# Gram chains of images 1 to 5: which engine runs the small operations (four convolution layers on one Trainium2 core)

## The chip, the cores and the metric

The kernel runs on one core of a Trainium2 chip. Its engines each have their own queue of instructions: TensorE (PE in the profile) multiplies matrices, VectorE (DVE) and ScalarE (ACT) work element by element, GpSimd (POOL) does so too and starts DMAs, SyncE (SP) starts most DMAs. The metric is the device time of one execution in microseconds (us); the smaller the better. Times are medians of several runs.

## The reference

The input `x` is 16 images of 64 channels of 128 x 128 pixels, in float32. Four layers follow each other, each with a group normalization `_gn` (32 groups of two channels) and an addition to its own input:

```python
def _L0_conv_ref(x, conv_w):
    xf = x.reshape(B, C, N)
    gram = jnp.einsum('bcn,bdn->bcd', xf, xf) / N
    y = jnp.einsum('bcd,bdn->bcn', gram, xf)
    out = jnp.einsum('oc,bchw->bohw', conv_w, y)
...
x = x + _L0_conv_ref(_gn(x), L0_conv_conv_w)            # a 64 x 64 Gram matrix of each image
x = x + _L1_conv_ref(_gn(x))                            # |Sobel x| + |Sobel y| of each channel
x = x + _L2_conv_ref(_gn(x), L2_conv_W, L2_conv_b)      # 3x3 convolution after a shift by a column
x = x + _L3_conv_ref(_gn(x), w_bin, w1x1, ...)          # 3x3 and 1x1, batch norm, leaky ReLU, clip
```

The batch norm of the last layer takes its mean over all 16 images, so its end can only be computed when all images are through.

## The kernel before, in words

One partition of the chip's memory stands for a channel of one half of an image (64 channels x upper and lower half = 128 partitions). Layer 0 is linear in `x`: once the Gram matrix of an image is known, normalization, Gram product, 1x1 weights and the residual become one 64 x 64 matrix `abd` and a few columns `co`. So an image passes through these stages:

- `Gram` (L407): loads the whole image (`xr`), rearranges it on ACT (`xw`), and sums 128 small products on PE into `pg`, a 64 x 65 Gram matrix with the channel sums.
- `gram_chain` (L301): about forty small operations on 128x1 to 128x128 tiles that turn `pg` into `abd` and `co`. It alternates between DVE, which computes, and PE, which sums over partitions by small products into one PSUM tile, `bank`.
- `Front`: applies `abd` (`po`), normalizes on ACT (`xh`), and does layer 1's Sobel filters on DVE: eight operations of about 1000 elements a step, with two absolute values (`Abs`, in place on `u` and `e`) on ACT between them.
- `Layer2` and `Layer3`: the convolutions on PE (`one`, `two`), differences `d` of rows and the final additions on DVE (`two`, `x`, `y`), twins `qd` of the differences. In layer 2, POOL starts the DMAs that make `qd`, scales the edge columns (`edges`, four operations) and zeroes columns of `v` (two operations); DVE's next `d` needs that `v`.
- at the end, 16 images are read again, normalized by the batch norm, added and written. This end is bound by DMA.

The stages run at the same time on different images. The program writes out the order by hand: a loop over steps, each in four quarters `q`, and in each quarter it calls the stages in turn (Layer3, Layer2, Front, Gram). At the end of the quarter `tick()` advances the chains: a chain is a generator, and each `yield` ends a link, so that a link's products on PE wait for operations that were queued one quarter earlier. Image 1's chain has fewer breaks (`if b > 1: yield`), so that some of its products stand right behind the operations that they need.

Every instruction goes into its engine's queue in the order in which the program names it, and the wrapper `InOrder` forbids the scheduler to move it:

```python
def __getattr__(self, name):
    call = getattr(self.engine, name)
    def ordered(*args, **kwargs):
        return self.tc.keep_in_program_order(call(*args, **kwargs))
    return ordered
```

Because of this wrapper nearly all instructions carry line L73, and the profile is read by tile names.

The Gram stages of images 1 to 6 run at double pace (`half`, L874), while the pipeline still fills: image 0's chain falls at 38 us, that of image b at step 12 + 4b, and layer 2 joins at step 23, layer 3 at step 34. `EARLY` is 3. The links that matter, with the queue that they stand in:

- `gs`: copy of `pg`, in the quarter in which ACT copies the first two `xw` pieces of the next image.
- `vv`: five columns made of the mean `mu` of a channel and the group's `mean` (the latter in `me`); PE's next product `bank<-kc,vv` reads them.
- `rw`: copy of a 2 x 256 product out of PSUM.
- `rc`: the 1x1 weights times `r`; `cs`: sums of PSUM and `g`; PE multiplies `rc` by `cs`.
- `r2`, `wbd` (in two 64 x 64 halves), `ad`, `abd`: they make the matrix; in the profile `r2` appears as `r<-r`.
- `co`: five small operations that make the columns for `Front`.

Of the kernel before, what the change touches and what calls it, by code (L numbers as in the profile page):

```python
# [12 lines left out]
ALU = mybir.AluOpType  # L13
# [9 lines left out]
EARLY = 3  # L23
# [85 lines left out]
def tile_kernel(ctx: ExitStack, tc: tile.TileContext, x, cw_h, w2_t, b2, wbin_t, w1_t, b1, gamma, beta, consts, out):  # L109
    nc = tc.nc  # L110
    pe, dve, act, sp, pool = (InOrder(tc, e) for e in (nc.tensor, nc.vector, nc.scalar, nc.sync, nc.gpsimd))
# [9 lines left out]
    def k(name):  # L121
        return kc[:, AT[name][0]:AT[name][1]]

    def load_const(src, shape, name):
        t = cpool.tile(shape, F32, name=name)
        nc.sync.dma_start(t, src)
        return t

    cwh = load_const(cw_h, [P, C], "cwh")
# [39 lines left out]
    def sv(name, n=1):  # L169
        return small.tile([P, n], F32, tag=name, name=name)  # L170
# [6 lines left out]
    def small_product(dst, wt, src):  # L177

        for o in (1 - last[0], last[0]):
            pe.matmul(dst[cols(o)], wt[:, cols(o)], src, start=True, stop=True)  # L180
        last[0] = o
# [5 lines left out]
    def sm(n, rows=P):  # L187
        if n > 8:
            return bank[0:rows, P:P + n]
        turn[0] = (turn[0] + 1) % 16  # L190
        return bank[0:rows, 8 * turn[0]:8 * turn[0] + n]
# [9 lines left out]
    wbd = wpool.tile([P, P], F32, name="wbd")  # L201
# [55 lines left out]
    def rstd(mE, eps):  # L257

        me = sv("me", 2)
        dve.tensor_copy(me, mE)  # L260
        nv = sv("nv")
        dve.scalar_tensor_tensor(nv, me[:, 0:1], me[:, 0:1], me[:, 1:2], op0=ALU.mult, op1=ALU.subtract)
        var = sv("var")
        dve.tensor_scalar(var, nv, -1.0, eps, op0=ALU.mult, op1=ALU.add)
        sd = sv("sd")
        act.activation(sd, var, AF.Sqrt)
        yield
        r0 = sv("r0")
        dve.reciprocal(r0, sd)

        e = sv("e")
        dve.scalar_tensor_tensor(e, var, r0, r0, op0=ALU.mult, op1=ALU.mult)
        dve.tensor_scalar(e, e, -0.5, 1.5, op0=ALU.mult, op1=ALU.add)
        r = sv("r")
        dve.tensor_mul(r, r0, e)
        return r, me[:, 0:1]
# [23 lines left out]

    def gram_chain(b, pg):  # L301

        gs = stp.tile([P, C + 1], F32, tag="gs", name=f"gs_{b}", bufs=1)
        dve.tensor_copy(gs, pg)
        if b > 1:
            yield
        gd = sm(C + 1)
        small_product(gd, k("same"), gs)
        yield
        g = stp.tile([P, C + 1], F32, tag="g", name=f"g_{b}", bufs=1)  # L310
        dve.tensor_scalar_mul(g, gd, 1.0 / HW)
        mu = g[:, C:C + 1]
        st = sv("st0", 2)
        dve.tensor_copy(st[:, 0:1], mu)
        junk0 = stp.tile([P, C], F32, tag="junk0", name=f"junk0_{b}", bufs=1)
        dve.scalar_tensor_tensor(
            junk0, g[:, 0:C], 1.0, k("Id"), op0=ALU.mult, op1=ALU.mult, accum_out=st[:, 1:2]
        )
        if b > 1:
            yield  # L320
        pm = sm(2)
        small_product(pm, k("gavg"), st)
        yield
        r, mean = yield from rstd(pm, GN_EPS)

        vv = sv("vv", 5)
        dve.tensor_scalar_mul(vv[:, 0:1], mu, -1.0)
        dve.tensor_sub(vv[:, 1:2], mu, mean)
        dve.tensor_copy(vv[:, 2:3], mu)
        dve.tensor_sub(vv[:, 3:4], mu, mean)  # L330
        dve.tensor_scalar_mul(vv[:, 4:5], mean, -1.0)
        if b > 1:
            yield
        pr = sm(2 * P, rows=2)
        pe.matmul(pr[:, 0:P], vv[:, 0:2], k("hsame"), start=True, stop=True)
        pe.matmul(pr[:, P:2 * P], vv[:, 2:4], k("hsame"), start=True, stop=True)
        yield
        rw = stp.tile([2, 2 * P], F32, tag="rw", name=f"rw_{b}", bufs=1)
        dve.tensor_copy(rw, pr)
        if b > 1:  # L340
            yield
        pc = sm(C)
        pe.matmul(pc, rw[:, 0:P], rw[:, P:P + C], start=True, stop=True)
        yield

        cs = stp.tile([P, 2, C], F32, tag="cs", name=f"cs_{b}", bufs=1)
        for s in range(2):
            dve.tensor_add(cs[:, s, :], pc, g[:, 0:C])
        rc = stp.tile([P, C], F32, tag="rc", name=f"rc_{b}", bufs=1)
        dve.tensor_scalar(rc, cwh, r, 0.5, op0=ALU.mult, op1=ALU.mult)  # L350
        csf = cs.rearrange("p s c -> p (s c)")
        if b > 1:
            yield
        pq = sm(C)
        small_product(pq, csf, rc)
        yield
        r2 = sv("r2")
        dve.tensor_mul(r2, r, r)
        for s in range(2):
            rows = slice(s * C, (s + 1) * C)  # L360
            dve.tensor_scalar_mul(wbd[rows, rows], pq[rows], r2[rows])
        ad = stp.tile([P, C], F32, tag="ad", name=f"ad_{b}", bufs=1)
        dve.scalar_tensor_tensor(ad, pq, r2, k("Id"), op0=ALU.mult, op1=ALU.add)
        abd = stp.tile([P, P], F32, tag="abd", name=f"abd_{b}", bufs=EARLY + 3)
        dve.tensor_add(abd, wbd, k("I"))
        if b > 1:
            yield
        pd = sm(C + 3)
        small_product(pd[:, 0:C], csf, ad)
        small_product(pd[:, C:C + 2], abd, vv[:, 2:4])  # L370
        small_product(pd[:, C + 2:C + 3], wbd, vv[:, 4:5])
        yield
        pp = stp.tile([P, 2, C], F32, tag="pp", name=f"pp_{b}", bufs=1)
        for s in range(2):
            dve.tensor_mul(pp[:, s, :], pd[:, 0:C], ad)
        av = sv("av", 3)
        dve.tensor_copy(av, pd[:, C:C + 3])
        if b > 1:
            yield
        pk = sm(1)  # L380
        small_product(pk, pp.rearrange("p s c -> p (s c)"), k("q"))
        yield
        bias = sv("bias")
        dve.tensor_copy(bias, av[:, 2:3])
        st1 = sv("st1", 2)
        dve.tensor_add(st1[:, 0:1], av[:, 0:1], bias)
        t = sv("t1")
        dve.scalar_tensor_tensor(t, av[:, 1:2], av[:, 1:2], pk, op0=ALU.mult, op1=ALU.subtract)
        dve.scalar_tensor_tensor(
            st1[:, 1:2], st1[:, 0:1], st1[:, 0:1], t, op0=ALU.mult, op1=ALU.subtract  # L390
        )
        if b > 1:
            yield
        pm = sm(2)
        small_product(pm, k("gavg"), st1)
        yield
        r, mean = yield from rstd(pm, GN_EPS)

        co = stp.tile([P, 4], F32, tag="co1", name=f"co1_{b}", bufs=EARLY + 3)
        dve.tensor_copy(co[:, 0:1], r)  # L400
        dve.tensor_sub(co[:, 1:2], bias, mean)
        dve.tensor_mul(co[:, 1:2], co[:, 1:2], r)
        dve.reciprocal(co[:, 2:3], r)
        dve.tensor_copy(co[:, 3:4], mean)
        lead[b] = abd, co

    class Gram:  # L407
# [5 lines left out]
        def at(self, i, q):  # L413
# [29 lines left out]
            if n == 6:  # L443
                chains.append(gram_chain(b, self.pg))
# [466 lines left out]
    for step in range(steps):  # L911
        for q in range(4):
# [13 lines left out]
            for b in range(B):  # L926
                at, n = pace[b]
                for m in range(n):
                    v = 4 * n * (step - at) + n * q + m
# [103 lines left out]
```

## Time and profile before

| | us |
|---|---|
| median of 3 runs | 2819.88 (2819.15 to 2820.23) |
| the profiled execution | 2818.68 |
| its span, first to last instruction | 2816.9 |

| engine | busy us | share of the span |
|---|---|---|
| PE | 2237.6 | 79% |
| DVE | 2201.0 | 78% |
| ACT | 2121.1 | 75% |
| POOL | 887.5 | 32% |

The page also cuts the span into 40 slices of 70.4 us; each digit is the busy share in tenths.

```profile
PE   4568899999999999999999999999999995000000
DVE  3999999898989898989898989999997435333332
ACT  4666779888888888888888888998997668333332
POOL 1035433343434343434343434454444310000000
PEclk7679999999999999999999999999999998555555
```

How to read it: an average over the whole span hides the stages. In the first five slices the pipeline fills: PE and ACT have gaps and DVE has hardly any. From the sixth slice to about the thirty-third PE is full. The rest is the end that DMA bounds. In other views each row of the timeline gives the start, the duration, the engine, the operation and `out<-in`, and in brackets the idle time of that engine before it with the one that ended it.

### The profile page before, as it was taken

How to read it: one execution, taken by the hardware profiler on the slowest of the kernel's cores; microseconds unless marked ns; L12 is line 12 of the kernel's file. 1: busy time of each engine (PE TensorE's matmuls, PEld its weight loads, DVE VectorE, ACT ScalarE, POOL GpSimd, SP SyncE). 2: the span in 40 equal slices, each digit the busy share in tenths (PEclk: the TensorE clock that was granted, in tenths of full speed). 3: DMA queues.
4: the chain of work that ended last, by engine and by line, in shares of the span. 5: the costliest groups of instructions: out<-in, count | busy, mean ns of one | idle time of the engine just before them, and what ended most of it. 6: DMA issues, size and time to landing. Idle time of an engine off the chain costs nothing. (4 is left out here: it accounts for less than half of the span.)

```text
span 2816.9 us, 46299 instructions
## 1 busy us (share of the span) xinstructions
PE 2237.6 (79%) x14772; PEld 1153.6 (41%) x14772; DVE 2201.0 (78%) x3758; ACT 2121.1 (75%) x3171; POOL 887.5 (32%) x1326
## 2 busy tenths in 40 slices
PE   4568899999999999999999999999999995000000
PEld 2323444545554545353635363466666542000000
DVE  3999999898989898989898989999997435333332
ACT  4666779888888888888888888998997668333332
POOL 1035433343434343434343434454444310000000
PEclk7679999999999999999999999999999998555555
DMA  6789978888888888888888877787877767999999
GB/s 167 193 221 228 236 192 241 214 229 207 229 208 225 217 220 215 219 218 218 217 219 213 226 182 193 206 212 202 216 207 189 208 195 266 419 420 420 420 420 391
DMA packets 688880, 685.95 MB, mean 244 GB/s; under 512 B 61744, under 2 KB 590144, under 8 KB 688640
## 3 DMA queue, kind: packets, MB, share of 16 engines
q1 hardware_dynamic: 662656, 614.42, 73.6%
q0 software_dynamic: 24576, 68.12, 9.9%
q8 instruction: 119, 1.95, 0.3%
q14 instruction: 121, 0.99, 0.1%
q10 hardware_dynamic: 1408, 0.46, 0.1%
HBM read 346.23 MB, written 268.44 MB: 218 GB/s over the span
## 5 line engine op out<-in xcount | busy, mean ns | idle before, releaser
L73 PE MATMUL two<-d,w 128*64 128x508 f32 (+2 forms) x2560 | 889.8, 586 | 0.0
L73 PE MATMUL two<-d,wi 128*64 128x508 f32 (+3 forms) x1536 | 618.4, 577 | 0.0
L73 POOL DMA_DIRECT2D qd<-d x512 | 270.3, 530 | 867.1 <-issue 324.6
L73 PE MATMUL two<-qd,pk 128*64 128x512 f32 (+1 forms) x1024 | 518.9, 588 | 3.7 <-DMA qd<-d 3.0
L73 POOL TENSOR_SCALAR edges<-v,co 64x8 f32<-64x8 f32 x512 | 353.9, 691 | 357.5 <-ACT v L73 244.8
L73 PEld LDWEIGHTS two<-d,w 128*64 128x64 f32 x2560 | 303.3, 136 | 281.0 <-issue 200.3
L73 PE MATMUL po<-x,abd 128*64 128x512 f32 x1024 | 368.9, 631 | 60.6 <-ACT xh L73 60.6
L73 DVE TENSOR_TENSOR d<-v 128x512 f32<-128x512 f32 (+1 forms) x512 | 346.3, 679 | 75.5 <-issue 36.3
L73 PE MATMUL one<-v,w 128*64 128x508 f32 (+2 forms) x1600 | 391.8, 578 | 0.0
L73 PE MATMUL one<-v,wi 128*64 128x508 f32 (+3 forms) x1536 | 390.1, 593 | 0.0
L73 ACT COPY qd<-d 64x512 f32<-64x512 f32 x512 | 315.2, 616 | 21.0 <-DVE d L73 14.5
L73 DVE SCALAR_TENSOR_TENSOR e<-e 128x1032 f32<-128x1032 f32 (+1 forms) x256 | 313.0, 1223 | 0.0
L73 ACT ACTIVATE xh<-po,co 128x128 f32<-128x128 f32 (+1 forms) x480 | 275.3, 621 | 39.3 <-PE po L73 37.2
L73 PEld LDWEIGHTS two<-d,wi 128*64 128x64 f32 x1536 | 194.6, 135 | 146.2 <-issue 100.2
L73 DVE SCALAR_TENSOR_TENSOR y<-two,c 128x1024 f32<-128x1024 f32 x128 | 155.9, 1218 | 122.8 <-ACT v L73 65.8
L73 POOL TENSOR_SCALAR v<-v,kc 128x9 f32<-128x9 f32 x256 | 247.3, 980 | 12.0
L73 PEld LDWEIGHTS one<-v,w 128*64 128x64 f32 x1600 | 169.4, 137 | 160.4 <-issue 99.5
L73 ACT ACTIVATE v<-x,co 128x512 f32<-128x512 f32 (+2 forms) x368 | 234.8, 704 | 0.0
L73 PEld LDWEIGHTS one<-v,wi 128*64 128x64 f32 x1536 | 162.3, 138 | 154.9 <-issue 113.0
L73 ACT ACTIVATE u<-u 128x1024 f32<-128x1024 f32 x128 | 135.5, 1058 | 97.3 <-DVE u L73 96.8
L73 DVE SCALAR_TENSOR_TENSOR u<-xh 128x1170 f32<-128x1170 f32 x128 | 175.5, 1371 | 12.2 <-ACT xh L73 9.8
L73 PEld LDWEIGHTS pg<-xw 128*64 128x64 f32 x4096 | 161.6, 143 | 46.4 <-issue 38.6
(154 smaller groups left out, 3424.7 us busy)
## 6 DMA issues: line engine op xcount, KB each, us to landing
xr<-in_x SPq DMA_DIRECT2D x128, 512.0 KB, 6.9
x<-in_x SPq DMA_DIRECT2D x256, 256.0 KB, 4.2
x_d<-u SPq DMA_DIRECT2D x512, 128.0 KB, 3.6
y_d<-y SPq DMA_DIRECT2D x512, 128.0 KB, 4.2
x_d<-x SPq DMA_DIRECT2D x496, 128.0 KB, 2.5
qd<-d POOLq DMA_DIRECT2D x256, 130.0 KB, 3.0
qd<-d POOLq DMA_DIRECT2D x256, 129.8 KB, 3.7
v<-x_d SPq DMA_DIRECT2D x448, 72.1 KB, 3.0
```

Of the source, the lines that this page charges most:

```text
L73: return self.tc.keep_in_program_order(call(*args, **kwargs))
```

## The change

For images 1 to 5 (`fill`), sixteen of the small operations of each chain leave DVE. What reads PSUM goes to ACT (`gs`, `rw`, the two halves of `wbd`), what reads only SBUF goes to POOL (five for `vv`, `r2`, `rc`, `abd`, four of the five for `co`): these are operations whose result DVE itself does not read in the same link. `ad` reads `r2`, so `r2` is computed one link earlier, next to `rc`; this move alone applies to all 16 images. The number of products on PE and the bytes that are moved stay the same.

```diff
     def gram_chain(b, pg):
 
+        fill = 1 <= b < 2 * EARLY
+        v, copy = (pool, act.copy) if fill else (dve, dve.tensor_copy)
         gs = stp.tile([P, C + 1], F32, tag="gs", name=f"gs_{b}", bufs=1)
-        dve.tensor_copy(gs, pg)
+        copy(gs, pg)
...
-        dve.tensor_scalar_mul(vv[:, 0:1], mu, -1.0)
-        dve.tensor_sub(vv[:, 1:2], mu, mean)
-        dve.tensor_copy(vv[:, 2:3], mu)
-        dve.tensor_sub(vv[:, 3:4], mu, mean)
-        dve.tensor_scalar_mul(vv[:, 4:5], mean, -1.0)
+        v.tensor_scalar_mul(vv[:, 0:1], mu, -1.0)
+        v.tensor_sub(vv[:, 1:2], mu, mean)
+        v.tensor_copy(vv[:, 2:3], mu)
+        v.tensor_sub(vv[:, 3:4], mu, mean)
+        v.tensor_scalar_mul(vv[:, 4:5], mean, -1.0)
...
-        dve.tensor_copy(rw, pr)
+        copy(rw, pr)
...
+        r2 = sv("r2")
+        v.tensor_mul(r2, r, r)
         rc = stp.tile([P, C], F32, tag="rc", name=f"rc_{b}", bufs=1)
-        dve.tensor_scalar(rc, cwh, r, 0.5, op0=ALU.mult, op1=ALU.mult)
+        v.tensor_scalar(rc, cwh, r, 0.5, op0=ALU.mult, op1=ALU.mult)
...
-        r2 = sv("r2")
-        dve.tensor_mul(r2, r, r)
         for s in range(2):
             rows = slice(s * C, (s + 1) * C)
-            dve.tensor_scalar_mul(wbd[rows, rows], pq[rows], r2[rows])
+            if fill:
+                act.mul(wbd[rows, rows], pq[rows], r2[rows])
+            else:
+                dve.tensor_scalar_mul(wbd[rows, rows], pq[rows], r2[rows])
...
-        dve.tensor_add(abd, wbd, k("I"))
+        v.tensor_add(abd, wbd, k("I"))
...
-        dve.tensor_copy(co[:, 0:1], r)
-        dve.tensor_sub(co[:, 1:2], bias, mean)
-        dve.tensor_mul(co[:, 1:2], co[:, 1:2], r)
+        v.tensor_copy(co[:, 0:1], r)
+        v.tensor_sub(co[:, 1:2], bias, mean)
+        v.tensor_mul(co[:, 1:2], co[:, 1:2], r)
         dve.reciprocal(co[:, 2:3], r)
-        dve.tensor_copy(co[:, 3:4], mean)
+        v.tensor_copy(co[:, 3:4], mean)
```

## The prediction

> **What bounds the kernel now.** I read the table of stages first, because the change touches only the chains of images 1 to 5, which by their copies of `gs` start at 80.6, 127.7, 176.0, 235.0 and 296.2 us. Columns: stretch, busy us and (instructions) of PE, PEld, DVE, ACT, POOL, then PE clock, DMA share, GB/s.
>
> ```profile
> 60.00:165.00 105.00, 57.55 (x704) 30.65 (x706) 98.70 (x167) 69.86 (x99) 0.41 (x2) 0.63 0.73 182
> 165.00:340.00 175.00, 145.70 (x1340) 67.24 (x1338) 162.70 (x328) 121.71 (x173) 94.60 (x114) 0.90 0.94 241
> 340.00:480.00 140.00, 138.54 (x952) 63.25 (x950) 131.86 (x251) 121.24 (x191) 53.55 (x83) 1.00 0.81 211
> 480.00:2340.00 1860.00, 1846.92 (x11356) 967.49 (x11354) 1628.26 (x2798) 1610.16 (x2527) 729.14 (x1114) 1.00 0.81 212
> ```
>
> To 340 us VectorE (DVE) sets the pace (94 and 93% busy) and GpSimd (POOL) has room; from 340 us TensorE (PE) does (99%). What is gained or lost before 340 us should therefore move everything behind it. The second view is the waits of PE between 60 and 345 us: who it waited for, us in total, times, longest.
>
> ```profile
> PE po L73 <- ACT xh L73: 45.1, 19, 6.2
> PE bank L73 <- DVE vv L73: 12.1, 4, 5.7
> PE bank L73 <- DVE rc L73: 4.4, 3, 2.0
> ```
>
> PE already stands still for `vv` and `rc`, two of the results that change engine. So I looked at the timeline around image 3's `vv`, first POOL (the small columns merge equal instructions), then DVE, then PE.
>
> ```profile
> 196.22 1.03 POOL L73 DMA_DIRECT2D qd<-d  x2 [4.52 <-issue]
> 197.28 7.34 POOL L73 TENSOR_SCALAR edges<-v,co 64x8 f32<-64x8 f32 x4
> ...
> 196.56 0.14 DVE L73 TENSOR_SCALAR vv<-me 128x1 f32<-128x1 f32 x1
> 196.62 1.23 DVE L73 SCALAR_TENSOR_TENSOR u<-u 128x1040 f32<-128x1040 f32 x1
> 197.77 1.23 DVE L73 SCALAR_TENSOR_TENSOR e<-e 128x1032 f32<-128x1032 f32 x1
> 198.91 1.22 DVE L73 TENSOR_TENSOR u<-u 128x1024 f32<-128x1024 f32 x1
> 200.05 1.22 DVE L73 SCALAR_TENSOR_TENSOR e<-e 128x1024 f32<-128x1024 f32 x1
> ...
> 205.38 0.69 DVE L73 TENSOR_TENSOR d<-v 128x512 f32<-128x512 f32 x1 [1.32 <-POOL v L73]
> ...
> 208.43 0.38 DVE L73 TENSOR_TENSOR two<-two,edges 128x8 f32<-128x8 f32 x2
> ...
> 196.56 1.01 PE L73 MATMUL bank<-kc,vv 128*2 128x128 f32 x4 [3.25 <-DVE vv L73]
> ```
>
> And four single `edges` instructions of POOL, all of one shape (min/median/max in ns, start):
>
> ```profile
> L73 POOL TENSOR_SCALAR edges<-v,co x1: 4157/4157/4157, 197.3 to 197.3; 64x8 f32<-64x8 f32 x1
> L73 POOL TENSOR_SCALAR edges<-v,co x1: 1212/1212/1212, 201.5 to 201.5; 64x8 f32<-64x8 f32 x1
> L73 POOL TENSOR_SCALAR edges<-v,co x1: 314/314/314, 204.3 to 204.3; 64x8 f32<-64x8 f32 x1
> L73 POOL TENSOR_SCALAR edges<-v,co x1: 4164/4164/4164, 257.0 to 257.0; 64x8 f32<-64x8 f32 x1
> ```
>
> The same 8 elements cost POOL 0.31 us while DVE is idle, 1.2 us beside one of DVE's large operations, and 4.2 us when four of them stand back to back, as in every Sobel step.
>
> **What the Trainium skill says.** "SBUF — State Buffer", section "Who interferes with whom": DVE and GpSimd share one port pair under an exclusive lock; a DVE operation with two SBUF inputs keeps out a GpSimd one that reads SBUF, and the later one waits in full. The trace agrees (0.31 against 4.2 us; the four DVE operations from 196.62 read two SBUF inputs each). On the other side DVE is not visibly slowed: 1.23 us for `e<-e` at 73.43 with POOL idle and at 197.77 with POOL waiting. "PSUM — Partial Sum Buffer", section "Engine vs sequencer instructions": the queues of ScalarE, VectorE and GpSimd are strict FIFO, and matmuls complete in order; PE's 3.25 us of waiting with 27 products behind it agrees.
>
> **The change part by part.** *Removed from DVE*, by start-to-start times of image 3: `gs` 0.13, five `vv` 0.33, `rw` 0.33, `rc` 0.15, `r2` with the two halves of `wbd` 0.87, `abd` 0.21, three of `co` 0.27: 2.29 us a chain, 11.4 us for five. For images 1, 4 and 5 DVE's wait for `pg` (1.01, 1.00, 0.69 us) leaves with `gs`.
>
> *Added to ScalarE (ACT)*: `gs`, `rw`, two halves of `wbd`. The nearest rows, 128x128 from PSUM at 0.45 us and 64x128 SBUF to SBUF at 0.29, give about 0.35, 0.5 and 2 x 0.35, an estimate: 1.6 us a chain. ACT idles 30% of this stretch, so mostly hidden, with two exceptions. `gs` goes behind the next image's first two `xw` copies. For image 1 they end at 84.15, and its chain has no break before the product `gd`, so DVE's `g`, now at 83.29, comes at about 84.95: +1.7 us, where DVE would have won 1.2. For image 2 ACT runs without a gap from 132 us to the Abs that DVE awaits at 136.95 (1.47 us idle): +0.3. Images 3 to 5: `gd` waits for `me` of the chain before in any case (to 179.34, 240.13, 301.78), so nothing is lost; but DVE's `two` at 237.68 and 299.32 needs PE's products of just then, so little is won.
>
> *Added to POOL*, twelve small operations a chain: five `vv`, `r2`, `rc`, `abd`, four of `co` less the reciprocal. The trace has no 128x1 operation on POOL; bounds are 0.31 us (free) and 4.2 (behind a Sobel block). Image 1 has an empty POOL queue, and DVE idles 1.27 us before 90.19, so `vv` fits in there. For image 2 PE has slack. Together images 1 and 2: -0.4 (2.1 won, 1.7 lost) and -1.9 (2.2 won, 0.3 lost), -2.3 us.
>
> From image 3 on POOL also serves layer 2. The order of its queue puts `vv` behind the two `qd` DMAs of the same quarter and ahead of four `edges` and two `v`. Image 3: the DMAs end at 197.25, inside the block. First `vv` 4.1 us, to 201.1 (the block starts 0.33 earlier); the next two 1.2 us each, to about 203.6; then DVE has run dry (203.99 less 0.66) and the fourth, the last that the product needs, takes 0.31 and 0.07 between: 204.0. PE starts at 204.1 instead of 196.56, 7.5 us late. Behind it in PE's order stand 12 products `one` and 20 `two`, the last at 206.09 taking 0.59: they now end at 214.2. DVE reads them at 208.43 and cannot before 214.3: +5.9 us, with the savings in that stretch already in it. (DVE's wait for `v`, 1.32 us now, grows too, but under this one.) `rc`: POOL's DMAs end at 212.33, `r2` takes 2.4 us and `rc` 1.2 in the block, so PE's product goes from 211.24 to about 216.0, its `two` end at 223.4, against DVE's read at 222.47: +1.1. `abd` comes while PE is still at `two`, hidden. Less 0.3 for `co`: +6.7 us.
>
> Image 4 likewise: DMAs end at 256.97; `vv` to 264.0, PE 7.7 us late (256.28), `two` end 273.4 for a read at 268.15: +5.3. `rc`: 272.06 plus 3.5 and 1.2, PE 5.9 us late (270.96), `two` end about 286.9 for a read at 284.04: +2.9. Less 0.4: +7.8 us.
>
> Image 5: PE's product stands at 319.57 and PE has no idle time from there on. POOL gets one `vv` in during DVE's small operations, the second waits for the block from 320.97, and the last comes when DVE runs dry, near 329: PE 9.7 us late at the entry of the stretch that it bounds. Some comes back (DVE's savings of 0.7, and PE's own waits later): I take +8, between 4 and 10. Its `rc` and `abd` then come before PE's turn, hidden.
>
> Sum: -2.3 + 6.7 + 7.8 + 8 = +20.2 us on the profiled execution, 2818.68 us (span 2816.9). The median, 2819.88, lies 1.2 higher, so 2840.
>
> **Rivals.**
> *Relief without a price: faster.* If POOL's 128x1 operations slip in at 0.31 + 0.07 us each, four `vv` cost 1.5 us after 197.25 and PE starts at 198.9; the `two` end at 209.0, about when DVE arrives. Then DVE's 2.29 us a chain count for images 1 to 4 (9.2), plus 1 us of `pg` waits, less 2 us of ACT's delays: 2811.7. For it: DVE's 93%, and that some `edges` did get in at 0.31. Against it: those fell in DVE's small operations, and exactly these leave DVE with the change. It decides if PE is less than about 1.7 us late at `vv`, the distance from 206.7 to 208.43.
> *Cover and price cancel: no change.* If one `vv` gets in at each DVE boundary (1.2 us, four to 202.1), images 3 and 4 lose some 4 us each, `rc` nothing; with image 5's loss absorbed by PE's waits and images 1 and 2 at -2.3 that is +5: 2825.
> *Worse.* PE ran at 0.90 of its clock in this stretch; 12 `one` took 4.90 us after the long wait at 196.56 and 2.79 at 211.56. If each longer wait costs 2 us more in five places, and `abd` delays its product by 2 in two of them: 2854.
>
> **How the numbers follow.** A difference below 0.2% (5.6 us) can't be told from none. The forecast with the worse case has 0.80, cancelled 0.08, relief 0.12. Cancelled sits at the upper edge of "same"; that and its neighbours give 0.07 same, 0.11 faster, 0.82 slower. The forecast's own range is 2828 to 2854: +8 with each `vv` at 1.2 us and image 5 at +4, +34 with the worse case. Reaching down to the cancelled case, 2823 to 2855.
>
> **What would show it.** In the profile after: PE waiting for POOL `vv` and `rc`, 6 to 10 us at a time for images 3 to 5; single `vv` on POOL of 1.2 to 4 us; a new DVE wait `two` for PE of 4 to 6 us; DVE's share between 165 and 340 us falling and that stretch longer by 12 to 15 us, nothing changed after 480 but its start. It is wrong if `vv` ends within 2 us of the DMAs, if PE makes up image 5's delay before 480 us, or if ACT's new copies, not POOL's, are what PE waits for.

## The result and the profile after

The changed kernel takes 2833.4 us (median of 4 runs, 2832.43 to 2834.43) against 2819.99 us (2819.15 to 2820.23, also 4 runs) for the kernel before, run beside it: a ratio of 1.0046, with a 95% interval of 1.0033 to 1.0059. It is slower, by about 13 us. The profiled execution took 2834.43 us (span 2832.6), 15.75 us more than that of before.

The table of stages of the changed kernel, with the same columns as before:

```profile
60.00:165.00 105.00, 58.20 (x678) 30.88 (x680) 93.94 (x135) 70.91 (x106) 13.18 (x22) 0.61 0.73 182
165.00:340.00 175.00, 130.53 (x1285) 62.57 (x1284) 145.57 (x270) 109.74 (x161) 98.81 (x136) 0.86 0.88 222
340.00:480.00 140.00, 140.00 (x956) 67.72 (x956) 126.77 (x240) 120.44 (x192) 52.88 (x89) 0.99 0.79 207
480.00:2340.00 1860.00, 1847.03 (x11365) 976.58 (x11360) 1639.49 (x2811) 1614.41 (x2530) 731.85 (x1125) 1.00 0.81 212
```

In the second stretch DVE falls from 162.70 to 145.57 us busy and PE from 145.70 to 130.53: in these 175 us both do less, so both were waiting longer. In the third, PE is full from end to end; in the fourth the two profiles hardly differ. The waits of PE between 60 and 345 us say for what (total us, times, longest):

```profile
PE po L73 <- ACT xh L73: 39.1, 18, 5.8
PE bank L73 <- POOL vv L73: 21.1, 7, 4.8
PE bank L73 <- POOL rc L73: 10.2, 2, 5.6
PE bank L73 <- DVE me L73: 7.6, 3, 4.2
PE bank L73 <- ACT gs L73: 6.9, 2, 4.7
```

Before, `vv` stood at 12.1 and `rc` at 4.4 us, both on DVE; the wait for ACT's `gs` is new, and falls in images 1 and 2 alone. DVE's waits in the same window grow from 21.8 to 44.0 us in sum. One wait of 9.8 us for ACT's `xh` is the same in both kernels; the largest new ones are these:

```profile
DVE d L73 <- issue: 14.5, 4, 5.7
DVE ad L73 <- ACT wbd L73: 4.0, 2, 2.5
DVE ad L73 <- POOL v L73: 2.5, 1, 2.5
```

(The last row is image 4's `ad`, at 291.99 us; ACT's `wbd` ends 0.1 us before it, later than POOL's `v`, so it is the same wait as in the row above.)

The timeline around image 3 shows both steps. First POOL, then DVE, then PE of the changed kernel:

```profile
196.70 1.03 POOL L73 DMA_DIRECT2D qd<-d  x2 [4.50 <-issue]
197.75 0.35 POOL L73 TENSOR_SCALAR vv<-g 128x1 f32<-128x1 f32 x1
198.08 1.12 POOL L73 TENSOR_TENSOR vv<-g,me 128x1 f32<-128x1 f32 x1
199.15 1.19 POOL L73 COPY vv<-g 128x1 f32<-128x1 f32 x1
200.31 1.17 POOL L73 TENSOR_TENSOR vv<-g,me 128x1 f32<-128x1 f32 x1
...
216.68 0.97 POOL L73 TENSOR_TENSOR r<-r 128x1 f32<-128x1 f32 x1
217.64 2.34 POOL L73 TENSOR_SCALAR rc<-cwh,r 128x64 f32<-128x64 f32 x1
```

```profile
202.82 1.28 DVE L73 SCALAR_TENSOR_TENSOR u<-e,co,u 128x1024 f32<-128x1024 f32 x1
...
209.67 0.69 DVE L73 TENSOR_TENSOR d<-v 128x512 f32<-128x512 f32 x1 [5.56 <-issue]
...
212.72 0.38 DVE L73 TENSOR_TENSOR two<-two,edges 128x8 f32<-128x8 f32 x2
...
223.65 0.28 DVE L73 SCALAR_TENSOR_TENSOR ad<-bank,r,kc 128x64 f32<-128x64 f32 x1 [2.50 <-ACT wbd L73]
...
227.31 0.69 DVE L73 TENSOR_TENSOR d<-v 128x512 f32<-128x512 f32 x1 [2.15 <-issue]
```

```profile
199.26 0.58 PE L73 MATMUL bank<-kc,vv 128*2 128x128 f32 x2 [4.83 <-POOL vv L73]
201.53 0.59 PE L73 MATMUL bank<-kc,vv 128*2 128x128 f32 x2 [1.69 <-POOL vv L73]
202.05 4.97 PE L73 MATMUL one<-v,wi 128*64 128x512 f32 x12
206.86 0.59 PE L73 MATMUL two<-d,wi 128*64 128x512 f32 x1
...
208.56 1.02 PE L73 MATMUL two<-d,wi 128*64 128x508 f32 x4
...
220.03 0.48 PE L73 MATMUL bank<-rc,cs 128*64 128x64 f32 x4 [5.57 <-POOL rc L73]
```

Each `vv` gets in at one boundary between two of DVE's large operations, about 1.15 us apart, so PE's last pair starts at 201.53 instead of about 197. Behind it in PE's queue stand `one` and `two`. DVE may write the next `d` only when the `two` products that read the half it overwrites are done; these products start at 206.86, later than DVE's last Sobel operation ends. Those that read this half are over with the row that ends at 209.58, and `d` starts at 209.67, while the other half is still being read. The idle time carries "issue" as its end because the profile names no single engine for it; that it is PE follows from these times, and from the runs below, where `d` no longer waits once PE's products come in time.

The same bookkeeping by images on these two executions, from the start of DVE's first Sobel operation (`u<-xh`, 128x1170) of the same step in both traces. Before, these steps start at 190.9, 235.2, 296.4 and 368.7 us:

| stretch | shift at its end, us | added in it | predicted |
|---|---|---|---|
| images 1, 2 | +0.5 | +0.5 | -2.3 |
| image 3 | +7.2 | +6.8 | +6.7 |
| image 4 | +14.4 | +7.1 | +7.8 |
| image 5 | +17.9 | +3.5 | +8 |
| to the end | +15.75 (whole execution) | -2.1 | 0 |

### The profile page after: what moved, and what is told of

Read it like the earlier page. It is cut to its first block, busy times and chain, and to the rows that moved or that the text cites. A ratio compares the mean times of both kernels' runs of the same rounds, so it can differ in the third digit from the quotient of the medians.

```text
span 2832.6 us, 46311 instructions
## 1 busy us (share of the span) xinstructions
PE 2240.7 (79%) x14772; PEld 1168.7 (41%) x14772; DVE 2190.5 (77%) x3678; ACT 2125.6 (75%) x3191; POOL 906.5 (32%) x1386
## 5 line engine op out<-in xcount | busy, mean ns | idle before, releaser
L73 POOL TENSOR_SCALAR edges<-v,co 64x8 f32<-64x8 f32 x512 | 329.1, 643 | 315.2 <-ACT v L73 256.5
```

## The experiments

Times are compared through the ratio to the kernel before that ran beside it on the same chip; its median was 2820.12, 2821.86, 2820.31, 2821.94 and 2820.98 us in five such groups of runs, and its single executions scattered from 2817.97 to 2827.51, so 0.1% of one profiled execution says nothing.

**One part taken back at a time.** Four variants of the changed kernel. `vv` on DVE again (the edit is the same in all five lines):

```diff
-        v.tensor_scalar_mul(vv[:, 0:1], mu, -1.0)
+        dve.tensor_scalar_mul(vv[:, 0:1], mu, -1.0)
...
```

> The changed kernel with only the five vv operations back on VectorE. Theory A (GpSimd delivers vv late, TensorE's product and the products behind it come late, and VectorE's difference d stands still until they have let go of its buffer): the two waits of 5.6 and 5.7 us of VectorE before d in images 3 and 4 go, against 5 x 0.33 us of vv work that returns: about 7 us less than the changed kernel, 2826 to 2828. Theory B (what costs is ScalarE: VectorE's ad waits for wbd there, and g for gs): at most 1 us less, 2832 to 2834.

Measured 2827.87 us (2826.14 to 2830.94), ratio 1.0027 (1.0017 to 1.0038). DVE's `d` in this run:

```profile
204.68 0.69 DVE L73 TENSOR_TENSOR d<-v 128x512 f32<-128x512 f32 x1 [1.31 <-POOL v L73]
...
218.66 0.29 DVE L73 SCALAR_TENSOR_TENSOR ad<-bank,r,kc 128x64 f32<-128x64 f32 x1 [2.50 <-ACT wbd L73]
222.30 0.69 DVE L73 TENSOR_TENSOR d<-v 128x512 f32<-128x512 f32 x1 [2.13 <-issue]
```

The wait of 5.56 us is gone, and the 1.3 us for `v` that was there before is back: this wait did come from `vv`. The second pair, `ad` and the `d` behind it, stays. Only a part of the loss went, though, as Theory A had expected (2826 to 2828).

The two halves of `wbd` on DVE again:

```diff
-            if fill:
+            if False:
                 act.mul(wbd[rows, rows], pq[rows], r2[rows])
```

> The changed kernel with only the two halves of wbd back on VectorE. Theory B: the four waits of 1.5, 2.5, 2.5 and 1.8 us of VectorE before ad go, 8.3 us, against some 3 us of wbd work that returns: 5 us less, about 2828. Theory A: in images 3 and 4 the late rc holds TensorE, so the wait moves from ad to the next d; only images 2 and 5 gain: 0 to 2 us less, 2831 to 2833.

Measured 2834.14 us (2831.92 to 2834.89), ratio 1.005 (1.0033 to 1.0067): nothing is won, a little less than Theory A had said and far from Theory B. The timeline of DVE shows why.

```profile
218.14 0.58 DVE L73 TENSOR_SCALAR wbd<-bank,r 64x64 f32<-64x64 f32 x2
218.74 0.28 DVE L73 SCALAR_TENSOR_TENSOR ad<-bank,r,kc 128x64 f32<-128x64 f32 x1
224.50 0.69 DVE L73 TENSOR_TENSOR d<-v 128x512 f32<-128x512 f32 x1 [4.26 <-issue]
```

`ad` no longer waits, and the next `d` waits 4.26 us where it waited 2.15. PE's products are as late as before, and DVE only meets them two instructions further on. In images 1 and 2, where DVE meets no such second wait, the same edit does help: the step that begins at 176.1 us comes 2.4 us earlier than in the kernel before, where the changed kernel has it 0.9 later. Of these 3.3 us, 1.5 are the wait at image 2's `ad` that is gone, and 1.9 were there already at the step that begins at 140.3 us. There ACT's copies had waited for a load, which let them start at 129.42 us in this execution and at 130.96 in that of the changed kernel.

ScalarE's part undone as a whole, and GpSimd's part undone as a whole:

```diff
-        v, copy = (pool, act.copy) if fill else (dve, dve.tensor_copy)
+        v, copy = (pool, dve.tensor_copy) if fill else (dve, dve.tensor_copy)
...
-            if fill:
+            if False:
                 act.mul(wbd[rows, rows], pq[rows], r2[rows])
```

> Only GpSimd's part of the change: vv, r2, rc, abd and co on GpSimd, while gs, rw and wbd stay on VectorE. Theory A: nearly the whole loss stays, 2829 to 2833. Theory B: no loss, 2815 to 2821.

Measured 2834.59 us (2831.88 to 2836.04), ratio 1.005 (1.0035 to 1.0065).

```diff
-        v, copy = (pool, act.copy) if fill else (dve, dve.tensor_copy)
+        v, copy = (dve, act.copy) if fill else (dve, dve.tensor_copy)
```

> Only ScalarE's part of the change: gs, rw and wbd on ScalarE, all the rest on VectorE. Theory A: within 3 us of the kernel before, 2817 to 2823. Theory B: most of the loss, 2828 to 2833.

Measured 2823.89 us (2817.95 to 2826.8), ratio 1.0011 (1.0004 to 1.0018). Both lie a little above what Theory A expects and well away from Theory B: GpSimd's part alone makes the whole loss, and ScalarE's alone about a quarter of it. That the two together are no slower than GpSimd's alone fits delays that overlap.

**`rc` besides `vv`, and alone.** Both on DVE (as in the first edit, and `dve` in place of `v` in front of `tensor_mul(r2, r, r)` and `tensor_scalar(rc, ...)`):

> vv, r2 and rc of images 1 to 5 go back to VectorE; GpSimd keeps abd and four of co, ScalarE keeps gs, rw and the halves of wbd. Theory A (the loss is what stands in GpSimd's queue between VectorE and TensorE: vv about 5.5 us by the run with vv alone, rc most of the rest): the time falls to that of the run with ScalarE's part alone, 2822 to 2825, and VectorE's waits at ad shrink or move. Theory B (the rest of the loss is VectorE waiting at ad for ScalarE's wbd, whatever rc does): stays at 2827 or above.

Measured 2819.06 us (2815.76 to 2823.24), ratio 0.9992 (0.9983 to 1.0): the whole loss is gone, a little more than Theory A had said. Theory B falls by the time alone: the slowest of the twelve executions took 2823.24 us. DVE still waits at `ad` in this variant (60 to 360 us):

```profile
DVE ad L73 <- ACT wbd L73: 7.1, 4, 2.4
```

But the execution profiled here is just that slowest one, 4.6 us longer than the one profiled of before, so these waits are not shown to cost nothing. `abd` and four of `co` still stand on GpSimd here, without a loss in the median. Why this variant reads lower than the one with ScalarE's part alone (1.0011), from which it differs by just these, no trace settles: the profiled executions of both are 6 us late at 386 us.

Only `r2` and `rc` back on DVE, `vv` left on GpSimd:

> Only r2 and rc of images 1 to 5 go back to VectorE; vv stays on GpSimd behind the DMAs. By the ratios of the runs so far, taking vv back gave 0.0019 (5.4 us) and taking rc back after it 0.0035 (9.9 us). Theory A with additive costs: ratio about 1.001, 2823 to 2825, and the vv delay alone is worth 5 us, rc's 10, where the prediction had 19 and 4. Rival F (the two delays overlap: whichever goes first brings little, since the other still leaves VectorE waiting): 1.002 to 1.003, 2826 to 2829, with the waits of 5.6 us at d of images 3 and 4 still there.

Measured 2827.1 us (2824.96 to 2830.07), ratio 1.0023 (1.0015 to 1.003), inside what Rival F expects, but with smaller waits than it says: at `d` in image 3 DVE waits 4.19 us, in image 4 3.29 us, against 5.56 and 5.67. That fits delays that overlap in part: `vv` is worth 0.0019 if it goes first and 0.0031 if it goes last (5.4 and 8.7 us), `rc` 0.0023 or 0.0035 (6.5 and 9.9 us). With intervals of about 0.001 to either side of each ratio, the times alone don't settle the overlap.

**The engine kept, the place changed.** `vv` stays on GpSimd but is issued one link earlier for images 1 to 5, as soon as `mean` is known; `rstd` calls it before its `yield`:

```diff
-    def rstd(mE, eps):
+    def rstd(mE, eps, early=None):
...
+        if early is not None:
+            early(me[:, 0:1])
...
-        r, mean = yield from rstd(pm, GN_EPS)
...
+        def means(mean):
+            v.tensor_scalar_mul(vv[:, 0:1], mu, -1.0)
...
+        r, mean = yield from rstd(pm, GN_EPS, means if fill else None)
+        if not fill:
+            means(mean)
```

> As the changed kernel, vv stays on GpSimd, but for images 1 to 5 it is issued one link earlier, as soon as mean is computed, a quarter of a step ahead of where it stood and so ahead of the qd DMAs of the next quarter. Theory A (its place in GpSimd's queue, behind the DMAs and inside the Sobel block, costs the time; not the engine): TensorE's waits for GpSimd vv fall below 1 us, VectorE's waits at d of images 3 and 4 (5.6, 5.7) fall to 1.3, 2825 to 2828. Theory C (GpSimd beside VectorE's operations costs the time wherever the instructions stand): 2831 or above.

Measured 2826.35 us (2823.88 to 2828.98), ratio 1.0014 (1.0008 to 1.0021). The waits at `d` of images 3 and 4 are 0.95 and 0.94 us. PE still waits once for 3.5 us for `vv`, in image 1, whose product has no break ahead of it. A new row appears among PE's waits, 8.7 us for `qd` in four places, which Theory A had not named: the DMAs now stand behind `vv`.

`r2` and `rc` one link earlier as well:

```diff
+        def weights():
+            v.tensor_mul(r2, r, r)
+            v.tensor_scalar(rc, cwh, r, 0.5, op0=ALU.mult, op1=ALU.mult)
+
+        if fill:
+            weights()
         yield
```

> As the one before, and r2 and rc too are issued one link earlier on GpSimd for images 1 to 5. Theory A: what is left of the loss is ScalarE's part, 2820 to 2824, with ad waits of up to 2 us. Theory C: 2829 or above.

Measured 2817.89 us (2814.09 to 2823.7), ratio 0.9985 (0.9977 to 0.9993): the loss turns into a small gain, more than expected. The same sixteen operations on the same engines; only their place in the queue differs.

Then `gs` and the halves of `wbd` back on DVE besides:

```diff
-        copy(gs, pg)
+        dve.tensor_copy(gs, pg)
...
-            if fill:
+            if False:
                 act.mul(wbd[rows, rows], pq[rows], r2[rows])
```

> vv, r2 and rc on GpSimd one link early, abd and four of co on GpSimd, of ScalarE's part only rw; gs and the halves of wbd back on VectorE. Theory A: neither engine is waited for at vv, rc, gs or ad, so some 1.2 us a chain of VectorE's time is really saved in images 1 to 4: 2814 to 2818, faster than the kernel before. Rival D (the small operations on VectorE stood in gaps that TensorE's or ScalarE's results leave anyway, so taking them away gives nothing): 2819 to 2822, the same as before.

Measured 2815.43 us (2811.8 to 2818.8), ratio 0.9976 (0.9967 to 0.9986). The interval overlaps that of the run before it, so what this last step gives is not shown.

**The place kept, the engine changed.** Does GpSimd earn anything, or only the early place? The last kernel with everything on DVE:

```diff
-        v, copy = (pool, act.copy) if fill else (dve, dve.tensor_copy)
+        v, copy = dve, dve.tensor_copy
```

> The place without the engine: the operations stand where the fastest variant so far has them (vv, r2 and rc one link early for images 1 to 5), but all on VectorE; nothing goes to GpSimd or ScalarE. Theory A (the fastest variant wins because VectorE's queue is shorter; the early place only keeps GpSimd's slower start from showing): 2818 to 2822, the same as before. Rival E (the early place is what wins, since TensorE waited for vv and rc in the kernel before too, 12.1 and 4.4 us, and GpSimd is no more than a bystander): about 2815 to 2817, as the fastest variant, and TensorE's waits for vv and rc fall below 3 us together.

Measured 2816.61 us (2813.57 to 2824.53), ratio 0.9986 (0.998 to 0.9993). This overlaps with the one before it, so the two ran once more, side by side:

> The kernel of the run before once more, beside the next one on one chip, to read the difference between the two directly. Rival E alone (the place wins, the engine gives nothing): the two within 1 us of each other. Theory A with E (the place gives some 4 us, and VectorE's shorter queue some 2 more): this one 1.5 to 4 us above the next.

> The fastest variant so far once more (early place; vv, r2, rc, abd and four of co on GpSimd, rw on ScalarE). Rival E alone: within 1 us of the one before. Theory A with E: 1.5 to 4 us below it, and below the kernel before by 5 to 7 us.

Measured 2816.93 us (2815.15 to 2819.01), ratio 0.9981 (0.9972 to 0.999), for the place alone, and 2813.14 us (2812.03 to 2814.51), ratio 0.9966 (0.9954 to 0.9979), for place and engine: 3.8 us apart, with ranges that do not meet. Both give something; "engine" here means GpSimd's twelve operations and `rw` on ScalarE together.

The variant with the place alone is 3.7 and 5.0 us faster than the kernel before in the two groups. Where that comes from is not shown. TensorE waited for `vv` before the change too, 12.1 us, and now waits 2.9:

```profile
PE po L73 <- ACT xh L73: 46.5, 17, 6.2
...
PE bank L73 <- DVE vv L73: 2.9, 1, 2.9
```

But other waits take their place: between 60 and 345 us the sum is 77.8 us before and 76.8 here. The step that begins at 368.7 us before comes only 0.8 us earlier in this execution, and 0.6 later in the first one of the same kernel. The rest is won after that, in the steady stretch, where all thirteen profiled executions with some part of the change gain 1.1 to 3.0 us on the one of before. What all thirteen share is `r2`, at least one link earlier for all 16 images; no run takes that move back alone. So a part of the 4 to 5 us may be due to `r2`, or to that one execution of before, and not to the place of `vv` and `rc`. The gain from the engines is there in time: the fastest kernel is 3.6 us ahead at that step in both its profiled executions.

And the timeline of image 3 in the fastest kernel, POOL, then PE:

```profile
190.24 0.62 POOL L73 TENSOR_SCALAR vv<-g 128x1 f32<-128x1 f32 x1
190.84 1.13 POOL L73 TENSOR_TENSOR vv<-g,me 128x1 f32<-128x1 f32 x1
191.91 0.18 POOL L73 COPY vv<-g 128x1 f32<-128x1 f32 x1
192.06 0.18 POOL L73 TENSOR_TENSOR vv<-g,me 128x1 f32<-128x1 f32 x1
192.21 0.21 POOL L73 TENSOR_SCALAR vv<-me 128x1 f32<-128x1 f32 x1
...
194.73 1.10 POOL L73 DMA_DIRECT2D qd<-d  x2 [2.31 <-issue]
```

```profile
192.03 0.65 PE L73 MATMUL bank<-kc,vv 128*2 128x128 f32 x4 [0.31 <-POOL vv L73]
```

`vv` is done before POOL's next DMAs instead of behind them, PE waits 0.31 us where it waited 4.83 and 1.69, and POOL even has 2.31 us left. This kernel beats the one before and the changed one: 0.9966 in the one group and 0.9976 in the other.

## Why the prediction was right or wrong

**What bounds the kernel and which way it goes: right.** DVE was the busiest engine up to 340 us, sixteen operations left it, and it became idle instead of faster: it met PE's late products. PE's waits for `vv`, forecast at 6 to 10 us an image, were 6.5, 5.9 and 5.2 us for images 3 to 5. The delay passed on almost whole to the stretch where PE is full.

**The place in POOL's queue: right, and shown.** The prediction put `vv` behind two DMAs, inside the Sobel block. With the same engine and an earlier place (ratio 1.0014 for `vv`, 0.9985 with `rc`) the loss vanishes. (The 27 products that the prediction names behind PE's wait of 3.25 us are 32, the 12 `one` and 20 `two` of its later count.)

**The price of `vv`: too high.** The step "first `vv` 4.1 us, the next two 1.2 us each" failed: it took the 4.16 us of the first `edges` for the price of a waiting operation. The first `vv` took 0.35 us and the others 1.12 to 1.19, so PE's last pair started at 201.53, not 204.1. This is the price that the rival "cover and price cancel" had assumed, one `vv` at each boundary. The shift of image 3 at the `vv` step was 3.8 us instead of 5.9, and of image 4 3.9 instead of 5.3.

**Where DVE meets PE: earlier than forecast.** Predicted was a wait at `two` of 4 to 6 us; it was 5.56 and 5.67 us, but at `d`, which stands ahead of DVE's `two` and needs only the first half of the same products. This hid a part of the error in the price: PE came to `one` 4.1 us late in image 3 instead of 7.5, which at `two` would have cost 2.4 us, and at `d` cost 3.8. The `v` wait said to grow under it did not show: POOL's `v` was zeroed by 205.8, long before.

**The price of `rc`: too low for image 3, right by chance for image 4.** Image 3 was to lose 1.1 us at this step and lost 3.6. PE's delay was forecast well: 216.0 us on the clock of before, and 220.03 less the 4.3 us already lost is 215.7, so PE was 4.5 us late. What was mis-sized lies behind it. The kernel before, then the changed one:

```profile
211.24 0.34 PE L73 MATMUL bank<-rc,cs 128*64 128x64 f32 x4 [1.38 <-DVE rc L73]
211.56 2.79 PE L73 MATMUL one<-v,wi 128*64 128x512 f32 x12
...
215.87 1.06 PE L73 MATMUL two<-d,wi 128*64 128x508 f32 x4
...
219.43 0.68 DVE L73 TENSOR_TENSOR d<-v 128x512 f32<-128x512 f32 x1
```

```profile
220.30 4.37 PE L73 MATMUL one<-v,wi 128*64 128x512 f32 x12
...
226.21 1.03 PE L73 MATMUL two<-d,wi 128*64 128x508 f32 x4
```

Before, `d` stood 2.5 us behind the end of the products it needs (216.9 us), and only so much could be hidden; the prediction counted from `two` at 222.47. And the twelve `one` took 4.37 us instead of 2.79: of the rival "worse", this much came true at this place, while behind image 3's `vv` they took 4.97 for 4.90. PE's 4.5 us, plus 1.6, less 2.5 gives the 3.6.

Image 4 was to lose 2.9 us and lost 2.7, after 1.6 us more that DVE had waited for PE's `two` between the images. Here two errors cancel: `r2` and `rc` took 2.4 us for the 4.7 forecast, so that PE's product came 3.5 us late and not 5.9, and `d` again had less cover than `two`.

DVE's wait of 2.50 us at `ad`, in the same step, was not forecast. `ad` does not only need PE's product; it follows ACT's `wbd`, and that stands behind ACT's own work:

```profile
221.91 1.11 ACT L73 ACTIVATE xh<-po,co 128x512 f32<-128x512 f32 x2
222.92 0.62 ACT L73 ACTIVATE wbd<-bank,r 64x64 f32<-64x64 f32 x2
```

`wbd` ends at 223.54 and `ad` starts at 223.65, though PE's product was there at 220.51. Both only read the same PSUM tile. The Trainium skill has a reason for such an order ("PSUM — Partial Sum Buffer", section "PSUM bank collisions raise a hardware error"): two engines must not be in one bank and quadrant (32 partitions) at the same time, reads included, and the compiler's scheduler adds a dependency between them. The trace agrees as far as the order goes; who added it here, no run shows. This wait does not set image 3's loss: with `wbd` on DVE the step lost 3.7 us without it, at `d`. It counts only where no later wait covers it. With `rc` back on DVE and `wbd` still on ACT, `d` waited for nothing there, `ad` waited 2.42 us, and the step lost 1.6.

Taken together, `vv` was forecast at 19.2 us (5.9 + 5.3 + 8) and `rc` at 4.0; the runs give 5.4 to 8.7 and 6.5 to 9.9. The two mis-sized terms have opposite signs, which is why images 3 and 4 agree so well in the table: part of that agreement is luck.

**Images 1 and 2: wrong sign.** The step "-0.4 and -1.9, -2.3 us" came out at +0.5. `gs` on ACT went as forecast: DVE's `g` at 85.35 for 84.95. What failed is that nothing was charged for ACT's `wbd`: 1.51 us at `ad` of image 2. Another 1.1 us came at the Abs ahead of 137.69 (2.59 instead of 1.47), where ACT's copies had waited for a load that landed 0.6 us later than before; nothing shows that the change did that. Without `wbd` on ACT the stretch came out at -2.5, helped by a load that landed early. These are single executions, and two of one kernel, the fastest, lie 1.5 us apart at this point.

**Image 5: half.** The step "PE 9.7 us late, +8" failed: POOL found DVE's small operations of a layer-3 chain just then and got `vv` in at 0.26, 0.20, 0.19 and 1.19 us. PE waited 4.50 and 0.68 us, and the stretch lost 3.5.

**The sum.** On the profiled executions +20.2 was forecast and +15.75 came: +2.8 from images 1 and 2, about -0.6 from 3 and 4, -4.5 from 5, and -2.1 further on, spread over the steady stretch, which the prediction had at zero. The one part of the change that reaches there is `r2`, one link earlier for all 16 images; all later variants keep it and show a like gain, and no run separates it from the scatter of the one execution of before. The time itself, 2833.4, lies in the range.

**The rival "relief without a price"** was right that there is something to win: with an early place the time does fall below the kernel before, to 0.9966. It was wrong that this comes with the place the change gives.

## What to carry to other kernels

Before moving small operations from a full engine to an idle one, read the target's queue at that very place: what stands ahead of them, and which of the first engine's operations run then; the idle share of the target says nothing. And see who waits for the result: here a product on PE with thirty others behind it, so that most of the delay came back to the engine that was to be relieved, as a wait at the next buffer. Look for the first instruction that meets such a wait: here it was `d`, with less cover than the `two` behind it. And try moving an operation earlier on its own engine first: of the 8.8 us that the fastest kernel won in its best comparison, 5.0 came without any change of engine, though which of the moved operations gave them is open.

## What the runs showed of the hardware

- A 128x1 operation on POOL took 0.18 to 0.22 us where it got in at once and 1.12 to 1.21 us where it had to wait for a boundary between two large DVE operations. `rc`, 128x64 with a scalar from a column, took 2.34 us there, two boundaries, and 0.31 us as the median of five once it stood earlier. Why `edges` waited for four boundaries (4.16 us) and these did not, no run shows.
- Among the windows in which POOL got in at 0.2 us are DVE's operations with one input in PSUM: in the fastest kernel three of `vv` ran one after the other from 191.91 to 192.42 us, while DVE was at `two<-two,edges` (191.84) and began `x<-two,c` (192.33). This agrees with the section of "SBUF — State Buffer" in the Trainium skill that the prediction names: a DVE operation with at most one SBUF input, outside the modes in which DVE uses two ports, does not contend with POOL. Others are runs of DVE's own small operations, as in image 5.
- DVE was not visibly slowed where POOL waited behind it: 1.23 us for `e<-e` at 197.93 us. It was slowed where POOL's operation was already running. In the changed kernel, `u<-u` at 100.38 us, beside POOL's 128x128 `abd` (100.15 to 100.77), took 1.47 us, where the median of its 128 is 1.22, and `e<-e` at 286.89, begun under POOL's `rc` (until 287.15), took 1.34 against 1.22.
